# One graph-attention and experts kernel on Trainium2: strides of the attention's values, work moved at three borders between stages, larger register loads

## The chip, the cores and the metric

The kernel runs on one core of one Trainium2 chip, as one launch. The metric is the device time of that launch in microseconds (us). The time before is 2967.96 us, the median of three runs (2966.99 to 2968.54).

The core's engines are named as in the profile: PE (TensorE matmul), PEld (TensorE weight load), DVE (VectorE), ACT (ScalarE), POOL (GpSimd), SP (SyncE, which only issues DMAs here). SBUF is the on-chip memory that the engines read, PSUM the one that PE writes to. Each engine works through its own instructions in order and waits on semaphores for the others.

## What is computed

Two layers on 4096 rows of 256 channels. Cut to what matters:

```python
# layer 0
x = x + gat(layernorm(x), adj, W0, a1, a2)          # 4 heads of 64 channels
h = layernorm(x)
for _ in range(30):
    h = h + 0.01 * tanh(h); h = h * sigmoid(h)
    h = layernorm(h) @ W.T + b
x = x + h
# layer 1: two attentions in a row, then 6 experts, the best 2 for each row
x = x + gat(gat(layernorm(x), adj, W1, A1), adj, W2, A2)
f = layernorm(x)
p = softmax(relu(f @ rw1 + rb1) @ rw2 + rb2)
top_w, top_i = top_k(p, 2); w = softmax(top_w)
x = x + sum_i w[i] * expert[top_i[i]](f)            # three matmuls with relu between

# gat, per head
e = leaky_relu(f1[:, None] + f2[None, :], 0.2)
out = elu(softmax(where(adj > 0, e, -inf)) @ h)
```

The three attentions are called layer 0, layer 1 and layer 2 below (tags g0, g1, g2).

## The kernel before

**Attention.** `attention()` runs three times. A softmax over exp(leaky_relu(f1 + f2)) is split by the sign of f1 + f2: on either side the exponential is a product of a row's factor and a column's, so the matmuls work on 0/1 masks as weights (fp8, `st` for edges with a positive sum, `below` for the others) and on *values*, which are the head's 64 channels times the column's factor, high and low halves in fp16, and the factor itself: 130 fp16 numbers. The rows of the graph are done in four chunks of eight tiles of 128, a chunk takes four heads, and a head takes eight steps of four column tiles. In each step ACT (L464) or DVE (L462) makes four signs, each of one column tile by the chunk's 1024 rows, DVE takes masks from them (L569, L575), and PE runs the matmuls at L521: for each of the 32 column tiles `j`, each of 8 row tiles and both parts, one weight load of a mask and one matmul of 130 columns over `values[:, j, h, part]`. That is 8192 for each attention. The order on DVE and ACT is written out by hand (L539).

The last argument of `attention()` is a pair: the stride between two rows of values in SBUF, in fp16 numbers (`2 * DV` is 130, so 260 bytes; 160 gives 320), and the stride between the two parts' sums in PSUM, in fp32 numbers. Before, it is (130, 130) in layer 0, (160, 130) in layer 1 and (130, 256) in layer 2. With 260 bytes, the second part of each pair starts at 4 past a multiple of 8 bytes.

Layer 0 also loads the adjacency, 64 pieces of 1 MB, makes its masks and stores them; layers 1 and 2 load the stored masks. Weights, `hs` and a column mean are prepared ahead of each attention (L125 to L155, L291 to L294, L430 to L435). There the mean is a matmul with a weight tile that holds 1/C, or the sums copied by POOL into a full tile (`xsb`, L432), in each of its columns.

**FFN.** 30 steps over 8 units of 512 rows make 240 slots, each working on six units at different stages: PE transposes (L869), DVE applies the last product's scale (L877) and thereby frees PE's banks, ACT does silu and halves (L893, L897), DVE the other half (L898), SP transposes the fp16 halves by DMA (L902), ACT does tanh (L907), POOL adds (L908) and takes the power for the norm's factor (L928), DVE takes statistics (L917, L919), PE multiplies (L937, L940). The order on PE, DVE, ACT and POOL is written by hand, that on SP is the planner's. The first eight slots also prepare the eight units: `measure` (DVE statistics), `rate` (ACT, then POOL's power at L760) and `init` (the scaling; L779 on DVE where it says True, else L782 on ACT). A table, `opening`, tells in which slot each comes. In mid-stage, at slots 32, 56, and so on, `load` or `load_apart` fetches each unit's rows of x1 again, 512 KB each, for the residual at the end. They need nothing but their buffer, and the planner put all eight on SP's queue at the opening, between the first transposes.

**Routing and experts.** `route(h)` works on one half of the rows: statistics (`over_std`, L101 to L106), normalised rows (L1114), which are also stored to `nd`, transposes and two small matmuls per group of 512 rows (L1101), then the ranking of the best two, the places of the rows in a list sorted by expert, and the list itself: `shift` (L1199), `seen`/`ex`/`expert` (L1238 to L1248, the expert of each tile), one-hot tiles (L1221, L1226) for a matmul that sorts, then `source` and `dest` (L1250 to L1260), from which POOL gathers and scatters. The weight sums `ws` come ahead of the list. The rows come through a ring of four buffers (L93). `route(0)` is done before the first tile of the experts, `route(1)` between tiles. The experts take 37 tiles of 128 rows for each half: gather (L1315), transposes (L1326), three matmul layers (L1354 twice, L1375), scatter (L1378). `fetch` copies the tile's first two weights with an index held in a register (L1346); the register is loaded from `expert` on PE, DVE and ACT for four tiles at a time (L1335). The end adds the two scattered results of each row to `acc`.

## Time and profile before

The profiled execution took 2983.79 us, and its span, from the first instruction to the last, is 2982.0 us at a mean granted clock of 0.98. That is 15.8 us above the median of the runs, so durations from the trace are of a slightly longer execution.

| Stage | From, us | To, us | What runs |
|---|---|---|---|
| layer 0, attention | 95.0 | 602.9 | 8192 matmuls at L521 |
| FFN, opening | 603 | 640 | first units, no full rhythm |
| FFN | 640 | 1600 | 3.92 us a slot |
| layer 1, attention | 1627.8 | 2108.7 | 8192 matmuls |
| layer 2, attention | 2161.1 | 2646.2 | 8192 matmuls |
| routing of the first half | 2646.5 | 2704.3 | until the first expert's matmul |
| experts | 2704.3 | 2956.4 | 74 tiles |
| end | 2956.4 | 2982.0 | last sums and stores |

Read the page from the top: the busy share of each engine over the whole span, then the slices, where each digit is the busy share of a fortieth of the span in tenths. The last field of a group's line is the idle time of its engine just before it, with what ended most of it. Times on PE are such that a matmul's own duration (219 ns for L521) overlaps with its neighbours; the step from one start to the next is what counts. The slices of PE's clock and of the DMA engines:

```profile
PEclk9999999989999999999999999999999999988998
DMA  9999885043333333333353032120302222142243
```

The clock is full nearly everywhere. The DMA engines are full only in the first sixth, where the adjacency is loaded, and half full about the end of the attentions.

### The profile page before, as it was taken

The page shows a single profiled execution, that of the slowest core. Times are in us where ns is not written, and L with a number is a line of the kernel's source. Part 1 is how long each engine was busy: PE and PEld are TensorE (multiplying, and loading weights), DVE is VectorE, ACT ScalarE, POOL GpSimd, SP SyncE. Part 2 cuts the span into 40 slices and gives each one's busy share as a digit, 9 for nine tenths or more (in the row PEclk, how much of TensorE's full clock was granted, in tenths as well). Part 3 has the DMA queues.
Part 4 walks back from the last instruction along what each step waited for, and adds up shares of the span by engine and source line. Part 5 has one row for each costly group of instructions (what it writes and reads, how often), then busy time and mean ns, then how long its engine had stood idle before and what let it go on. Part 6 is the DMA issues. An engine that isn't in the chain of part 4 may idle for free. (4 is left out here: it accounts for less than half of the span.)

```text
span 2982.0 us, 82665 instructions
## 1 busy us (share of the span) xinstructions
PE 2795.9 (94%) x33923; PEld 2553.5 (86%) x33923; DVE 2737.1 (92%) x5769; ACT 2463.9 (83%) x3125; POOL 1159.1 (39%) x1084
## 2 busy tenths in 40 slices
PE   7899999979999999999998999999899999977986
PEld 5799999968888888888887999999799999967885
DVE  7999999999999999999998899999889999976665
ACT  5799999978888888888877999999799999954332
POOL 3000000079999999999982000000300000015563
PEclk9999999989999999999999999999999999988998
DMA  9999885043333333333353032120302222142243
GB/s 281 274 258 242 230 234 159 25 126 69 68 69 68 68 67 70 68 67 70 68 110 119 26 99 72 49 87 27 108 27 94 66 94 94 31 141 93 79 165 133
DMA packets 484450, 320.07 MB, mean 107 GB/s; under 512 B 416589, under 2 KB 445418, under 8 KB 477930
## 3 DMA queue, kind: packets, MB, share of 16 engines
q1 hardware_dynamic: 474034, 290.27, 36.1%
q0 software_dynamic: 7104, 19.41, 2.1%
q8 instruction: 268, 4.39, 0.6%
q10 hardware_dynamic: 2936, 5.11, 0.5%
q14 instruction: 108, 0.88, 0.1%
HBM read 183.00 MB, written 52.04 MB: 79 GB/s over the span
## 5 line engine op out<-in xcount | busy, mean ns | idle before, releaser
L521 PE MATMUL acc<-vals,st 128*128 128x130 f16 x12288 | 1425.1, 219 | 39.0 <-DVE u L476 30.6
L521 PE MATMUL acc<-vals,below 128*128 128x130 f16 x12288 | 1424.7, 221 | 14.0 <-DVE below L575 13.2
L464 ACT ACTIVATE st<-f1b,nf 128x1024 int8<-128x1024 f32 x1265 | 1334.2, 1145 | 30.3 <-PE acc L521 19.8
L521 PEld LDWEIGHTS <-below 128*128 128x128 fp8e4 x12288 | 1185.9, 97 | 55.0 <-issue 42.6
L521 PEld LDWEIGHTS <-st 128*128 128x128 fp8e4 x12288 | 1207.2, 98 | 9.6 <-DVE st L569 7.8
L937 PE MATMUL po<-wT,zT 128*128 128x256 f32 x1920 | 576.2, 382 | 6.1 <-DVE y L877 3.5
L940 PE MATMUL po<-w,zT 128*128 128x256 f16 x3840 | 577.9, 273 | 0.5 <-DMA zT<-z 0.5
L908 POOL TENSOR_TENSOR th<-th,y 128x1024 f32<-128x1024 f32 x232 | 548.9, 2366 | 14.5 <-DVE z_st L917 0.4
L940 PEld LDWEIGHTS <-zT 128*128 128x128 f16 x3840 | 376.6, 98 | 161.7 <-DMA zT<-z 1.2
L575 DVE TENSOR_TENSOR below<-m,st 128x1024 int32<-128x1024 int32 x384 | 469.9, 1224 | 32.6 <-DVE st L569 0.9
L569 DVE TENSOR_TENSOR st<-st,m 128x1024 int32<-128x1024 int32 x384 | 466.8, 1216 | 0.2
L877 DVE SCALAR_TENSOR_TENSOR y<-po,z_rs,bias 128x256 f32<-128x256 f32 x928 | 384.3, 476 | 2.2 <-PE tp L869 0.7
L917 DVE BATCH_NORM_STATS2 z_st<-z 128x6 f32<-128x256 f32 x960 | 335.5, 412 | 0.0
L937 PEld LDWEIGHTS po<-wT,zT 128*128 128x128 f32 x1920 | 291.1, 192 | 15.6 <-issue 3.7
L893 ACT ACTIVATE z<-th 128x1024 f32<-128x1024 f32 x240 | 251.9, 1050 | 17.6 <-POOL th L908 16.8
L928 POOL TENSOR_TENSOR z_rs<-z_rs,mhalf 128x4 f32<-128x4 f32 x240 | 245.4, 1022 | 3.1 <-ACT z_rs L927 3.1
L907 ACT ACTIVATE th<-y 128x1024 f32<-128x1024 f32 x232 | 241.7, 1042 | 0.0
L924 ACT COPY zT<-tp 128x512 f32<-128x512 f32 x240 | 140.4, 585 | 90.6 <-PE tp L869 89.5
L462 DVE TENSOR_SCALAR st<-f1b,nf 128x1024 int8<-128x1024 f32 x271 | 201.0, 742 | 6.2 <-PE acc L521 6.2
L760 POOL TENSOR_TENSOR x_rs<-x_rs,mhalf 128x4 f32<-128x4 f32 x8 | 9.4, 1175 | 505.3 <-ACT x_rs L759 505.3
L1046 POOL IOTA along_i<- 128x512 int32 (+1 forms) x5 | 2.8, 557 | 485.8 <-PE acc L521 485.7
L439 POOL MEMSET hs<- 128x4 f32 x3 | 0.3, 103 | 485.9 <-DVE u L493 485.9
(263 smaller groups left out, 3158.5 us busy)
## 6 DMA issues: line engine op xcount, KB each, us to landing
ring<-in_adj_dram SPq DMA_DIRECT2D x64, 1024.0 KB
m<-edges SPq DMA_DIRECT2D x32, 1024.0 KB
f1b<-fd SPq DMA_DIRECT2D x48, 512.0 KB
edges<-m SPq DMA_DIRECT2D x16, 1024.0 KB
y<-yd SPq DMA_DIRECT2D x16, 512.0 KB
ew<-in_L_ffn_expert_w_dram SPq DMA_DIRECT2D x18, 256.0 KB
t<-in_x_dram SPq DMA_DIRECT2D x8, 512.0 KB
old<-in_x_dram SPq DMA_DIRECT2D x16, 256.0 KB
```

The lines of the kernel that those rows point to most:

```text
L464: nc.scalar.activation(out, f1, AF.Sign, bias=f2, scale=-1.0)
L521: nc.tensor.matmul(acc[:, i, part * apart_s : part * apart_s + 2 * DV], masked[part][:, at_i // TR, s, rows], values[:, j, h, part], start ...
L569: nc.vector.tensor_tensor(above, above, whole, OP.bitwise_and)
L575: nc.vector.tensor_tensor(below, whole, above, OP.bitwise_xor)
L877: nc.vector.scalar_tensor_tensor(t[:, r, :] if end else y[:, g * G + r, :], po[:, r, :], rstd[:, r : r + 1], t[:, r, :] if end else bias, ...
L893: ins = nc.scalar.activation(z, th.pop(u), AF.Silu, scale=0.01)
L907: nc.scalar.activation(th[at], was, AF.Tanh, scale=0.01)
L908: ins = (nc.gpsimd if at else nc.vector).tensor_tensor(th[at], th[at], was, OP.add)
L917: nc.vector.bn_stats(st[:, r, :], z[:, r, :])
L928: nc.gpsimd.tensor_tensor(rs[u], rs[u], mhalf, OP.pow)
L937: nc.tensor.matmul(po[:, r, :], src[:, r * P : (r + 1) * P], wT, start=True, stop=False)
L940: nc.tensor.matmul(po[:, r, :], src16[:, part * G + r, :], w16[:, other, :], start=False, stop=(part == 1 and other == 1),)
```

## The change

- Values in layer 0 have a stride of 132 numbers (264 bytes). Layer 2 gets layer 1's pair (160, 130): 320 bytes, and sums 130 apart instead of 256.
- The mean is kept as one column and broadcast where it is a weight tile. The copy `xsb` on POOL is gone; the matmul at L435 reads the sums by a broadcast.
- FFN opening: `init` of units 4 and 5 goes from DVE in slots 2 and 3 to ACT in slots 3 and 4, `rate` of both one slot earlier.
- The eight loads in mid-stage are made to follow the L898 of the slot before.
- Routing: the second half's rows are loaded straight into `acc`, two of the four loads before `route(0)`, and the statistics of these two are done in `route(0)`'s last two turns. `seen`, `ex` and `expert` come after `source` and `dest`, DVE's order in `route(0)` is as written, and the tiles `ew`, `acc` and `ws` are allocated in another order. With these, the planner now puts the weight sums later.
- Registers are loaded for 4, 17 and 16 tiles of each half instead of ten times: 6 loads on each engine instead of 20.

As further effects of the planner's order, SP issues four mask loads of layer 2 earlier, two signs on ACT and three mask operations on DVE come earlier there, and POOL's first power in the routing comes behind its integer tables.

```diff
-    mean = const.tile([P, P], F32, name="mean")
-    nc.gpsimd.memset(mean, 1.0 / C)
+    share = const.tile([P, 1], F32, name="mean")
+    nc.gpsimd.memset(share, 1.0 / C)
+    mean = share.to_broadcast([P, P])
...
-                    xsb = prep.tile([P, KC, P], F32, name="xsb")
-                    nc.gpsimd.tensor_copy(xsb, xt[:, :, None].to_broadcast([P, KC, P]))
                     pt = small_ps()
                     for k in range(KC):
-                        nc.tensor.matmul(pt[:, :C], xsb[:, k, :], w[:, k, :C], start=(k == 0), stop=(k == KC - 1))
+                        nc.tensor.matmul(
+                            pt[:, :C], xt[:, k : k + 1].to_broadcast([P, P]), w[:, k, :C], start=(k == 0), stop=(k == KC - 1)
+                        )
...
         {k: functools.partial(many, *v) for k, v in side.items()},
+        (132, 2 * DV),
     )
...
+        halved = []
         units = FFN_STEPS * NG
         opening = {
-            0: [(init, 2)],
-            1: [(rate, 4), (rate, 5), (init, 3, True)],
-            2: [(init, 4, True)],
-            3: [(init, 5, True), (measure, 6)],
-            4: [(rate, 6), (measure, 7)],
-            5: [(init, 6), (rate, 7)],
+            0: [(init, 2), (rate, 4), (rate, 5)],
+            1: [(init, 3, True)],
+            3: [(init, 4), (measure, 6)],
+            4: [(rate, 6), (init, 5), (measure, 7)],
+            5: [(rate, 7), (init, 6)],
             6: [(init, 7)],
         }
...
             if 0 <= g < NG and part == 0:
-                if g < NG // 2:
-                    load(g)
-                else:
-                    load_apart(x1d, g)
+                ins = load(g) if g < NG // 2 else load_apart(x1d, g)
+                follows(ins, halved[0], "in mid-stage, when the queue has room")
...
+                halved[:] = [lower]
                 zT16[u] = work.tile([P, 2 * G, P], F16, name="zT16", bufs=4)
                 nc.sync.dma_start_transpose(zT16[u], z16.rearrange("p s r c -> p (s r c)"))
...
-            (2 * DV, 256) if n else (160, 2 * DV),
+            (160, 2 * DV),
...
+        def rest(g):
+            return acc[:, (NGH + g) * G : (NGH + g + 1) * G, :]
+
+        def measure_other(g):
+            early[g] = over_std(rone, rest(g), f"_{g}")
...
             def load(g):
-                if h * NGH + g not in ahead:
-                    load_ahead(x3d, h * NGH + g, runs_of)
-                rows[g] = ahead.pop(h * NGH + g)
+                if h:
+                    rows[g] = rest(g)
+                    if g in early:
+                        stds[g] = early.pop(g)
+                    else:
+                        nc.sync.dma_start(rows[g], runs_of(x3d, NGH + g))
+                else:
+                    rows[g] = ahead.pop(g)
...
+                if not h and g >= NGH:
+                    measure_other(g - NGH)
...
-            seen = rone.tile([P, T, E - 1], F32, name="seen")
...
-            nc.vector.tensor_copy(expert[h], ex)
             lst = rone.tile([P, T, 2], F32, name="lst")
...
             nc.vector.tensor_copy(dest[h], df)
             yield
+            seen = rone.tile([P, T, E - 1], F32, name="seen")
...
+            nc.vector.tensor_copy(expert[h], ex)
...
+            for g in range(2):
+                nc.sync.dma_start(rest(g), runs_of(x3d, NGH + g))
             steps = route(0, turned, bank)
-            for _ in range(4):
-                next(steps)
+            with tc.manual_schedule(engines={mybir.EngineType.DVE}):
+                for _ in range(4):
+                    next(steps)
...
-            for _ in steps:
-                pass
+            with tc.manual_schedule(engines={mybir.EngineType.DVE}):
+                for _ in steps:
+                    pass
...
-                n = min(4, T - t)
+                n = 4 if t == 0 else min(-(-(T - 4) // 2), T - t)
```

More of the change, by code (lines that the diff above doesn't have):

```diff
@@ L92, in load_ahead, with over_std @@
         turns[0] += 1
-        queue.dma_start(t, view(src, g))
         ahead[g] = t
-    def over_std(pool, src):
+        return queue.dma_start(t, view(src, g))
+    def over_std(pool, src, mark=""):
         st = pool.tile([P, G, 6], F32, name="ln_st")
-        mv = pool.tile([P, G, 2], F32, name="ln_mv")
+        mv = pool.tile([P, G, 2], F32, name=f"ln_mv{mark}")
         for r in range(G):
@@ L103, in over_std @@
             nc.vector.bn_aggr(mv[:, r, :], st[:, r, :])
-        rstd = pool.tile([P, G], F32, name="ln_rstd")
+        rstd = pool.tile([P, G], F32, name=f"ln_rstd{mark}")
         nc.vector.tensor_scalar(rstd, mv[:, :, 1], EPS, None, op0=OP.add)
@@ L293, in greatest @@
                     pt = small_ps()
-                    nc.tensor.matmul(pt[:, : 2 * H], mean[: 2 * H], dm, start=True, stop=True)
+                    nc.tensor.matmul(pt[:, : 2 * H], share[: 2 * H].to_broadcast([2 * H, P]), dm, start=True, stop=True)
                     nc.vector.tensor_copy(mb[:, 0, :], pt[:, H : 2 * H])
@@ L740, in gnn_ffn_kernel, with load @@
     x1, measured, rates = {}, {}, {}
-    def load(g, queue=nc.sync):
-        if g not in ahead:
-            load_ahead(x1d, g, queue=queue)
+    def load(g):
+        ins = load_ahead(x1d, g)
         x1[g] = ahead.pop(g)
+        return ins
     def measure(g):
@@ L836, in load_apart @@
             x1[g] = hold.tile([P, G, C], F32, name="x1")
-            nc.sync.dma_start(x1[g], rows_of(src, g))
+            return nc.sync.dma_start(x1[g], rows_of(src, g))
         for g in range(4, NG):
@@ L1025, in gnn_ffn_kernel @@
         bT = one.tile([P, NB], F32, name="bT")
-        acc = one.tile([P, NT, C], F32, name="acc")
-        ws = one.tile([P, 2, NT], F32, name="ws")
         bsel = [one.tile([P, T, 2 * KC], F32, name=f"bsel{h}") for h in range(2)]
@@ L1031, in gnn_ffn_kernel @@
         source = [one.tile([P, T], I32, name=f"source{h}") for h in range(2)]
-        ew = [one.tile([P, E, KC, C], F32, name=f"ew{i}") for i in range(3)]
+        ew = [one.tile([P, E, KC, C], F32, name=f"ew{i}") for i in (2, 1, 0)][::-1]
+        acc = one.tile([P, NT, C], F32, name="acc")
+        ws = one.tile([P, 2, NT], F32, name="ws")
         b3 = one.tile([P, E, C], F32, name="b3")
@@ L1078, in over @@
             return t[:, :, None].to_broadcast([P, n, m])
+        early = {}
+        def rest(g):
+            return acc[:, (NGH + g) * G : (NGH + g + 1) * G, :]
+        def measure_other(g):
+            early[g] = over_std(rone, rest(g), f"_{g}")
         def route(h, turned, bank):
@@ L1094, in route @@
                     load(g + 2)
-                if g < NGH:
+                if g < NGH and g not in stds:
                     stds[g] = over_std(rwork, rows[g])
@@ L1238, in route @@
                 yield
-            seen = rone.tile([P, T, E - 1], F32, name="seen")
-            nc.vector.tensor_tensor(
-                seen,
-                along[:, :T, None].to_broadcast([P, T, E - 1]),
-                first[:, None, 1:].to_broadcast([P, T, E - 1]),
-                OP.is_ge,
-            )
-            ex = rone.tile([P, T], F32, name="ex")
-            nc.vector.tensor_reduce(ex, seen, axis=AX.X, op=OP.add)
-            nc.vector.tensor_copy(expert[h], ex)
             lst = rone.tile([P, T, 2], F32, name="lst")
@@ L1261, in route @@
             yield
+            seen = rone.tile([P, T, E - 1], F32, name="seen")
+            nc.vector.tensor_tensor(
+                seen,
+                along[:, :T, None].to_broadcast([P, T, E - 1]),
+                first[:, None, 1:].to_broadcast([P, T, E - 1]),
+                OP.is_ge,
+            )
+            ex = rone.tile([P, T], F32, name="ex")
+            nc.vector.tensor_reduce(ex, seen, axis=AX.X, op=OP.add)
+            nc.vector.tensor_copy(expert[h], ex)
             ohe = rone.tile([P, T, E], F32, name="ohe")
```

## The prediction

> **What bounds the kernel now.** I read the page first, then the busy time per stage, then two stages closely. The page says that no one engine is the answer for the whole:

> ```profile
> PE 2795.9 (94%) x33923; PEld 2553.5 (86%) x33923; DVE 2737.1 (92%) x5769; ACT 2463.9 (83%) x3125; POOL 1159.1 (39%) x1084
> ...
> L464 ACT ACTIVATE st<-f1b,nf 128x1024 int8<-128x1024 f32 x1265 | 1334.2, 1145 | 30.3 <-PE acc L521 19.8
> ...
> L940 PEld LDWEIGHTS <-zT 128*128 128x128 f16 x3840 | 376.6, 98 | 161.7 <-DMA zT<-z 1.2
> ```

> So it has to be read by stage. The stage view (columns: stretch, length, busy us of PE, PEld, DVE, ACT, POOL with counts, granted clock, DMA share, GB/s) for layer 0's attention, the FFN's opening, a steady FFN stretch, layer 2's attention, the routing, the experts:

> ```profile
> 95.00:603.00 508.00, 483.52 (x8192) 477.77 (x8192) 489.16 (x554) 480.30 (x491) 8.31 (x12) 0.99 0.72 198
> 603.00:640.00 37.00, 20.50 (x108) 14.57 (x106) 34.75 (x100) 27.09 (x44) 24.22 (x24) 0.72 0.59 164
> 1000.00:1040.00 40.00, 40.00 (x288) 32.76 (x287) 39.92 (x134) 35.09 (x52) 38.54 (x32) 1.00 0.33 72
> 2161.00:2646.00 485.00, 476.01 (x8188) 473.90 (x8188) 449.76 (x495) 446.94 (x452) 0.00 (x0) 0.99 0.21 64
> 2646.00:2704.00 58.00, 23.00 (x132) 15.13 (x130) 42.18 (x156) 18.54 (x27) 19.85 (x38) 0.68 0.56 193
> 2704.00:2956.00 252.00, 237.64 (x1739) 219.22 (x1737) 160.79 (x490) 97.31 (x233) 145.56 (x146) 0.99 0.33 107
> ```

> Layer 2 is PE's (476 of 485). Layer 0 has three engines near 485 of 508, and in its middle ACT is full (50.00 of 50 between 250 and 300 us). The opening is DVE's (34.75 of 37), and routing has PE idle for 35 of 58 us behind small serial DVE work. Experts are PE's again.

> **The strides (layers 0 and 2).** L521's matmuls alone, same columns, PE and PEld only; the second line is layer 1 (values at 320 bytes), the third layer 2 (260 bytes):

> ```profile
> 200.00:300.00 100.00, 96.36 (x1657) 95.45 (x1654) 1.00 0.89 245
> ...
> 1850.00:1950.00 100.00, 98.96 (x1741) 98.58 (x1739) 1.00 0.20 64
> ...
> 2300.00:2400.00 100.00, 99.25 (x1714) 98.76 (x1712) 1.00 0.26 81
> ```

> The step is 98.96/1741 = 56.8 ns at 320 bytes and 99.25/1714 = 57.9 at 260. At 260 bytes the two matmuls of a pair start at multiples of 4 and of 8 bytes in turn; from the starts in the trace the one takes 59.45 ns to the next, the other 55.84: 115.28 a pair, against 113.32 in layer 1. Layers 0 and 2 are alike there, though their sums stand 520 and 1024 bytes apart in PSUM, so the sums' stride that layer 2 gets costs nothing.
> *Layer 2* gets layer 1's form. Its heads run 29.97 us each, layer 1's 29.54; DVE and ACT have at most 28.5 of work a head. 16 x 0.43 = 6.9, so **-7.0**. Ends: -4.2 (the two whole loops, 485.1 less 480.9 us, if layer 1's waits come too) and -8.0 (4096 pairs x 1.96 ns).
> [...]
> *Layer 0* gets 264 bytes: every start a multiple of 8, not of 64, a form that no row shows. Layer 2's steps depend on nothing but 4 against 8, so I take 264 as good as 320 (ends 0 and 1.96 ns a pair). But ten of 16 heads last 31 to 33 us, which is ACT's 28.8 signs x 1.04 plus 1.8; they stay. The other six can give 0.5 each at most, with DVE at 29.6 to 30.6 in four of them: **-1.5** (0 to -4).

> **FFN opening.** Before, DVE does the scaling of units 4 and 5 itself:

> ```profile
> 617.05 3.37 DVE L779 TENSOR_SCALAR x<-x,x_rs,x_nm 128x256 f32<-128x256 f32 x4
> ...
> 630.02 1.62 DVE L877 SCALAR_TENSOR_TENSOR y<-po,z_rs,bias 128x256 f32<-128x256 f32 x4
> ```

> First column start, second length. Two such blocks (3.37 + 2.10) leave DVE, and L877, which frees PE's banks (PE waits 3.5 us for it), can come 3 to 5 us sooner. ACT takes them at 2.06 each, and its slot becomes 3.7 + 2.06 + 0.3 = 6.1 us against DVE's old 5.1 to 5.9, for about four slots: it gives back some 2. Two POOL rates come a slot earlier and lie in POOL's idle time. I take **-2.5** (+1 to -5).

> **Row loads in mid-stage.** Eight loads of 512 KB leave the opening, where SP issued them between the first transposes, and come one per 24 slots, each right before a transpose on SP's queue. A slot is 3.92 us; its transpose holds the DMA engines for about 1.4 (share 0.33), so 2.5 are free, and 512 KB at the 290 GB/s that this queue reaches take 1.8. PE waits for zT 1.2 us in the whole run. The new wait of SP (for the L898 of the slot before) has the next transpose behind it, which waits for a later L898 anyway. **0**; if the cover is gone, each load delays one transpose by up to 2 us, +16 at the worst.

> **Means as one column, xsb.** L435's weights are read from the sums directly. It waited for ACT, not for POOL's copy of 1.33 us, which hid beside it; a broadcast fp32 column already loads in 198 ns at L341 against 192 for a full tile at L305. Layer 2's opening ends with 4.7 us of waiting for `below` (DVE L575), which is prepared by DVE alone; neither edit touches it. **0** (-0.5 to +0.5).

> **Routing.** Up to 2683.9 the order is nearly kept; POOL's first power is moved behind its iotas, 2.2 us later, and the normalised rows, transposes and ping-pong behind it follow: +1.9. SP gets two 512 KB loads ahead of the expert weights; they wait for the last x3d rows and freed buffers, as the first expert weight did, with one nd write and all weights behind them: 3 us of queue, with 10 us free before the first gather. Then comes the chain to the gather's indices:

> ```profile
> 2683.93 0.34 DVE L1240 TENSOR_TENSOR seen<-along,first 128x185 f32<-128x185 f32 x1
> ...
> 2697.09 0.17 DVE L1259 TENSOR_SCALAR source<-sf 128x37 int32<-128x37 f32 x1
> ...
> 2696.88 1.01 POOL L106 TENSOR_TENSOR ln_rstd<-ln_rstd,mhalf 128x4 f32<-128x4 f32 x1 [33.16 <-DVE sf L1258]
> 2698.15 1.54 POOL L1315 DMA_INDIRECT gx<-nd,source  x1 [0.26 <-DVE ln_mv L103]
> ```

> Of these 13.2 us, `seen` to `expert` (0.9), sel and bsel (2.1), three copies of weights and the second half's statistics (2 to 3) move behind the indices; parts of them overlap: -2.8. The weight sums at the front move away, -0.6. The gather no longer stands behind L106 (-0.8), and what follows it saves 0.5. Statistics of two groups come into the loop's last turns, where DVE waits for PE. Sum **-2.8** (+2 to -6).

> **Experts.** A tile takes 2.87 us of PE; 74 tiles are 212 of the 252 us, another 13 are the second half's routing, the rest stalls. One group of that routing can now run before the first tile, in PE's idle time (-2.1), and the statistics of two groups leave the path (-0.5). Register loads fall from 20 to 6 on PE, DVE and ACT; L1335's rows show a median of 346 ns on DVE and 310 on ACT. 14 x 0.35 = 4.8 us leave DVE; about 2 of that stood before a tile: **-4.5** together (0 to -8). [...] In the trace one register takes 323 ns and four take 346 on DVE, 8 ns more each, so 17 should take 0.45. [...]

> **Sum.** -7.0 - 1.5 - 2.5 + 0 + 0 - 2.8 - 4.5 = -18.3. The profiled execution took 2983.8 us with a span of 2982.0, 15.8 above the median of 2967.96; this cuts from both alike: span about 2964, median **about 2950 us** (0.6% faster). A measurement of this kernel can tell 0.2%, about 6 us, from no change.

> **Rivals.**
> - *Only layer 2 carries* (0.22): the opening turns ACT-bound, routing gives +1.9 and takes it back, tiles meet the same stalls. For it: every other part moves work between engines that are each near full. Against: routing has idle time on all. -7 to -10: 2959.
> - *Layer 0 gains as layer 2 does* (0.15): its ACT heads would have to be paced by PE. For: PE's 483.5 of 508. Against: ACT at 50.00 of 50. -6.5 more: 2943.
> - *Slower* (0.08): the steady FFN falls into another rhythm. Its slots take 3.92 us (PE 40.00, DVE 39.92, POOL 38.54 of 40, no slack anywhere), while those just after the opening ran at 3.80, so the pace depends on how the units stand to each other, and the opening is what sets this. A slot of 4.03 us or more, 0.11 x 225 = 25 us, makes it slower; at 4.05 it is 2979. Against: the order of a steady slot is unchanged.
> - *The stride doesn't do what it says* in layer 0 (64-byte starts needed): 2951, inside the forecast.

> **How the numbers follow.** The forecast holds 0.55, with 2943 to 2957 of its own. The range 2937 to 2964 takes in layer 0's case and most of the first rival. Faster (below 2962): 0.55 + 0.15 + 0.12 of the first rival = 0.82; same: its other 0.10; slower: 0.08.

> **What would show it.** L521's step in layers 0 and 2 at 56.7 ns (57.9 in layer 0 would refute 264 bytes); layer 2's loop near 478 us; layer 0's still over 500 with ACT full; PE's wait for L877 in the opening gone; zT waits still about 1 us; `source` some 18 us behind the last lg (2697.1 against 2675.6 now); the large register loads under 0.6 us. A steady slot other than 3.92 us, zT waits of more than 5 us, or register loads of 3 us would make the prediction wrong.

## The result, and the profile after

The changed kernel takes **2959.28 us** (median of 15 runs, 2952.40 to 2963.02), the kernel before in the same rounds 2967.03 (2964.74 to 2971.78). The ratio is 0.9971, 95% interval [0.9963, 0.9979]: 7.75 us or 0.29% faster. The forecast was 2950, with 2943 to 2957 around it and an outer range of 2937 to 2964: the time lies in the outer range, but the change brought only two fifths of the 18.3 us that the sum had. The profiled execution took 2959.31 us, with a span of 2957.4.

That span is 24.6 us under the one shown of before, three times what the runs differ by. The experiments show why: of two chips on which the kernel before was profiled again, one spends some 17 us more in the experts alone, and the first profile has that mark. The experts' 251.7 us of before are therefore no measure. Layers 1 and 2, the FFN and the routing agree from chip to chip (480.9 and 481.0, 485.1 twice, 3.92 us a slot twice, 58.2 twice); layer 0's loop took 503.9 to 511.4 us from one profile to the next, whatever the kernel, so the 3.7 us by which it is shorter here are no measure either.

The page after, the same three lines (busy and share; two groups of section 5 with busy, mean ns, idle before them):

```profile
PE 2788.3 (94%) x33923; PEld 2546.6 (86%) x33923; DVE 2734.9 (92%) x5761; ACT 2467.3 (83%) x3133; POOL 1159.8 (39%) x1083
...
L465 ACT ACTIVATE st<-f1b,nf 128x1024 int8<-128x1024 f32 x1265 | 1333.2, 1142 | 30.3 <-PE acc L522 23.7
...
L941 PEld LDWEIGHTS <-zT 128*128 128x128 f16 x3840 | 376.2, 98 | 161.0 <-DMA zT<-z 0.9
```

PE has 7.6 us less of busy time, most of it layer 2's. The wait for zT did not grow (0.9 us against 1.2): the loads in mid-stage delay no transpose that PE waits for. By stage, in the order shown before (layer 0, opening, steady FFN, layer 2, routing, experts), with the same columns (stretch, length, busy us of PE, PEld, DVE, ACT, POOL with counts, granted clock, DMA share, GB/s):

```profile
94.00:599.00 505.00, 479.98 (x8190) 474.58 (x8191) 489.59 (x554) 480.29 (x491) 8.30 (x12) 0.99 0.72 199
599.00:636.00 37.00, 21.87 (x126) 15.79 (x124) 32.73 (x98) 34.37 (x58) 27.02 (x27) 0.77 0.37 79
1000.00:1040.00 40.00, 40.00 (x289) 32.87 (x287) 39.91 (x137) 34.50 (x52) 38.52 (x32) 1.00 0.44 83
2154.00:2634.00 480.00, 470.51 (x8190) 467.68 (x8189) 450.34 (x496) 444.66 (x451) 6.00 (x20) 0.99 0.21 65
2634.00:2688.00 54.00, 26.70 (x141) 16.99 (x139) 43.35 (x161) 17.15 (x27) 13.98 (x20) 0.71 0.60 207
2688.00:2930.00 242.00, 232.88 (x1729) 218.49 (x1727) 162.00 (x485) 98.80 (x233) 148.10 (x145) 0.98 0.34 111
```

In the opening DVE fell from 34.75 to 32.73 and ACT rose from 27.09 to 34.37 of 37. A steady FFN stretch is what it was. Layer 2 needs 480 us instead of 485. L522 (L521 before) alone, layers 0, 1 and 2:

```profile
200.00:300.00 100.00, 95.97 (x1653) 95.19 (x1651) 1.00 0.88 246
1850.00:1950.00 100.00, 98.97 (x1741) 98.58 (x1739) 1.00 0.19 60
2300.00:2400.00 100.00, 99.08 (x1735) 98.34 (x1733) 1.00 0.31 97
```

Layer 2 has layer 1's density now: 99.08/1735 = 57.1 ns, and from start to start 56.66 where PE runs on. **Layer 0 has not changed**: 95.97/1653 = 58.1, as 96.36/1657 before, and from start to start again 55.84 and 59.4 in turn.

The routing's chain to the gather's indices, its first line as it was before and then two lines of after; and the register loads, PE's as they were before and then those of after in the queues of the three engines (shortest, median and longest in ns, first and last start):

```profile
2683.85 0.17 DVE L1199 SCALAR_TENSOR_TENSOR shift<-first,ends 128x6 f32<-128x6 f32 x1
...
2670.02 0.17 DVE L1215 SCALAR_TENSOR_TENSOR shift<-first,ends 128x6 f32<-128x6 f32 x1
...
2681.11 0.15 DVE L1265 TENSOR_SCALAR source<-sf 128x37 int32<-128x37 f32 x1
```

```profile
L1335 PEldq TENSOR_LOAD <-expert x20: 312/332/519, 2685.6 to 2945.3; - x20
...
L1355 ACTq TENSOR_LOAD <-expert x6: 319/1674/3591, 2682.9 to 2875.3; - x6
L1355 DVEq TENSOR_LOAD <-expert x6: 359/1364/3808, 2683.0 to 2876.3; - x6
L1355 PEldq TENSOR_LOAD <-expert x6: 351/1443/4207, 2683.0 to 2874.5; - x6
```

From `shift` to `source` it is 11.1 us instead of 13.2 (2683.85 to 2697.09). The loads are the surprise: shortest, median and longest are 0.35, 1.4 and 4.2 us on PE, where before the median was 0.33. 6 loads take 12.05 us of PE's queue, 20 took 6.98.

### The profile page after: what moved, and what is told of

Same layout as the page of the kernel before. It is cut to its first block, busy times and chain, and to the rows that moved or that the text cites. A ratio compares the mean times of both kernels' runs of the same rounds, so it can differ in the third digit from the quotient of the medians.

```text
span 2957.4 us, 82630 instructions
## 1 busy us (share of the span) xinstructions
PE 2788.3 (94%) x33923; PEld 2546.6 (86%) x33923; DVE 2734.9 (92%) x5761; ACT 2467.3 (83%) x3133; POOL 1159.8 (39%) x1083
## 5 line engine op out<-in xcount | busy, mean ns | idle before, releaser
L522 PE MATMUL acc<-vals,st 128*128 128x130 f16 x12288 | 1416.3, 220 | 38.6 <-DVE u L477 31.1
L522 PE MATMUL acc<-vals,below 128*128 128x130 f16 x12288 | 1416.0, 221 | 13.3 <-DVE below L576 12.6
L465 ACT ACTIVATE st<-f1b,nf 128x1024 int8<-128x1024 f32 x1265 | 1333.2, 1142 | 30.3 <-PE acc L522 23.7
L522 PEld LDWEIGHTS <-below 128*128 128x128 fp8e4 x12288 | 1195.0, 97 | 55.4 <-issue 48.4
L522 PEld LDWEIGHTS <-st 128*128 128x128 fp8e4 x12288 | 1206.1, 98 | 8.7 <-DVE st L570 6.9
L877 DVE SCALAR_TENSOR_TENSOR y<-po,z_rs,bias 128x256 f32<-128x256 f32 x928 | 384.4, 476 | 2.2 <-PE tp L869 0.7
```

The source lines that it names most:

```text
L465: nc.scalar.activation(out, f1, AF.Sign, bias=f2, scale=-1.0)
L522: nc.tensor.matmul(acc[:, i, part * apart_s : part * apart_s + 2 * DV], masked[part][:, at_i // TR, s, rows], values[:, j, h, part], start ...
L877: nc.vector.scalar_tensor_tensor(t[:, r, :] if end else y[:, g * G + r, :], po[:, r, :], rstd[:, r : r + 1], t[:, r, :] if end else bias, ...
```

## The experiments

Three batches, each on one chip, always beside the kernel before. A label with a_ is an edit of the changed kernel, one with b_ of the kernel before; "best" puts parts of the change on the kernel before. Ratios are those of the measurement with their intervals, and can differ a little from the quotient of the two medians. "Routing" is from layer 2's last matmul to the first one of the experts, "experts" from there to PE's end, both from the profiles.

| Kernel | Batch | Time, us | Before there | Ratio, 95% interval | Layer 2's loop | Routing | Experts |
|---|---|---|---|---|---|---|---|
| b_again (one run) | 1 | 2985.28 | 2986.29 | | 485.1 | 58.2 | 253.9 |
| a_regs4 | 1 | 2969.67 | 2986.29 | 0.9949 [0.9937, 0.9961] | 479.3 | 54.2 | 251.2 |
| a_align (one run) | 1 | 2982.65 | 2986.29 | | 477.9 | 55.4 | 263.0 |
| a_open | 1 | 2985.53 | 2986.29 | 0.9999 [0.9991, 1.0007] | 478.1 | 53.8 | 264.7 |
| after_again | 2 | 2957.88 | 2967.90 | 0.9969 [0.9957, 0.9981] | 478.9 | 54.7 | 240.9 |
| a_regs8 | 2 | 2952.12 | 2967.90 | 0.9941 [0.9928, 0.9955] | 479.5 | 54.4 | 232.8 |
| a_regs_al | 2 | 2953.97 | 2967.90 | 0.9951 [0.9937, 0.9964] | 479.0 | 54.8 | 237.0 |
| b_route | 2 | 2960.10 | 2967.90 | 0.9975 [0.9966, 0.9984] | 485.2 | 55.3 | 232.9 |
| b_again2 (one run) | 3 | 2963.20 | 2968.32 | | 485.1 | 58.2 | 236.7 |
| b_l2 | 3 | 2961.62 | 2968.32 | 0.9978 [0.9969, 0.9987] | 478.2 | 58.2 | 236.8 |
| a_regs_off | 3 | 2957.97 | 2968.32 | 0.9967 [0.9956, 0.9978] | 479.5 | 54.0 | 239.2 |
| best | 3 | 2951.32 | 2968.32 | 0.9939 [0.9925, 0.9953] | 479.4 | 55.5 | 231.3 |

### The kernel before again: b_again and b_again2

No edit.

> The kernel before, unchanged, for a second profile. The first profiled execution was 16 us above the median of the runs. Theory A (the profile itself makes small stalls longer at the register loads, one every four or five tiles): again 2980 to 2986 us, with the experts' 28 or so longer tiles, 35 us in all. Rival B (that execution was an outlier somewhere else, such as in layer 0): about 2968, and layer 0's loop near 504 us as after the change, not 507.9.

> The kernel before once more, for a profile on the same chip as the three below. What took longer on the first batch's chip lay in the experts. Theory: attentions and FFN as always (508, 481, 485 us; slots 3.92), and routing plus experts, from layer 2's last matmul to PE's end, take 295 to 298 us where the kernel takes 2968, and 310 to 312 where it takes 2986. Rival: the chips differ in every stage alike.

Both theories of the first were wrong: profiling adds nothing, since the plain runs took 2986 there too, and layer 0 was 508.0 us. The second settled it: routing and experts together took 294.9 us, where 312.1 was read on batch 1's chip (its layer 0 was 504.1, not the expected 508). These are the experts of batch 1 and batch 3, the same program:

```profile
2703.00:2957.00 254.00, 237.07 (x1738) 219.22 (x1736) 160.15 (x491) 96.75 (x233) 145.39 (x146) 0.99 0.33 106
```

```profile
2698.00:2935.00 237.00, 232.04 (x1738) 218.04 (x1736) 163.49 (x491) 98.16 (x233) 146.29 (x146) 0.99 0.35 114
```

and who PEld waited for in them, in us, times, longest:

```profile
PEld ph L1354 <- DVE h L1367: 10.1, 9, 1.7
PEld ph L1354 <- issue: 10.1, 14, 2.0
```

```profile
PEld ph L1354 <- DVE h L1367: 4.1, 4, 1.5
PEld ph L1354 <- issue: 2.2, 9, 0.3
```

The work is alike; the stalls differ, half of them ("issue") with nothing in the trace that ends them. In layers 1 and 2 (480.9 and 485.1 us on one chip, 481.0 and 485.1 on the other) and the FFN (3.92 us a slot) there is none of it. The granted clock of the experts is 0.99 on both. What makes batch 1's chip slower there isn't settled. So experts are compared inside a batch, or between batches 2 and 3, where the kernel before took 2967.90 and 2968.32.

### Register loads: a_regs4, after_again, a_regs8, a_regs_al, a_regs_off

```diff
-                n = 4 if t == 0 else min(-(-(T - 4) // 2), T - t)       # 4, 17, 16
+                n = min(4, T - t)                                      # a_regs4
+                n = 4 if t == 0 else min(9 if t == 28 else 8, T - t)   # a_regs8
+                n = 4 if t == 0 else 16 if t == 4 else T - t           # a_regs_al: 4, 16, 17
+                n = 1 if t == 0 else min(4, T - t)                     # a_regs_off
```

> The changed kernel with registers loaded for four tiles at a time, as before (20 loads on each engine, not 6). My prediction's step (a load costs 0.35 us, hardly more for more registers): 2 to 5 us slower than the changed kernel, 2961 to 2964. Theory after seeing the trace (loads of 16 and 17 take 1.3 to 4.2 us on each engine, and stop three engines; the small ones were hidden): 3 to 8 us faster, 2951 to 2956.

> The changed kernel itself, timed beside the three below on one chip. On the chip of the first batch the kernel before took 2986 us and not 2967, and variants with the large register loads gained nearly nothing there. Theory (large loads cost 13 us in the routing and experts, the small ones did not): 2 to 7 us faster than the kernel before, routing and experts at 316 to 319 us. Rival (the first batch's chip was peculiar): 0.9971 again, routing and experts near 296 us.

> The changed kernel with register loads of 4, 8, 8, 8 and 9 for each half (10 loads on each engine; every start a multiple of 4 tiles, 16 bytes). If a load costs about 0.2 us for each register: 1.6 us each, and the time stands between the changed kernel's and that with fours. If the cost comes only from loads that start off 16 bytes, as the 16 registers from tile 21 do: under 0.8 us each, and the time is that with fours or 1 to 3 us better.

> The changed kernel with loads of 4, 16 and 17 (starting at tiles 4 and 20, both multiples of 16 bytes) in place of 4, 17 and 16 (starting at 4 and 21). In the changed kernel's trace 17 registers from tile 4 took 1.3 to 2.1 us and 16 from tile 21 took 3.4 to 4.2. If the start decides: both now 1.2 to 2 us, and the kernel is 4 to 8 us faster than the changed one. If it is the number of loads, or the tile where it falls: the second load again above 3 us, and no faster.

> The changed kernel with register loads of 1, then 4 at a time, so that every load of four starts 4 bytes past a multiple of 16. Theory (an aligned four is one access of some 0.3 us, single registers cost about 0.25 each): each load of four takes 0.9 to 1.1 us instead of 0.34, and the kernel is 3 to 10 us slower than with aligned loads of four or eight. Rival (long loads are slow for their length, not their start): 0.34 us each, no slower.

On batch 1's chip, fours made the changed kernel gain 16.6 us where a_open, with the large loads, gained nothing. Some 3.8 us of that are a_open's table of the opening (below); the experts alone are 251.2 us with fours against 263.0 (a_align) and 264.7 (a_open) with the large loads. On batch 2's chip the gap is smaller but plain: 2952.12 with eights, 2957.88 with the change's loads, experts 232.8 against 240.9. There the rival of after_again was right, and the theory drawn from batch 1 alone was not: 0.9969, with routing and experts at 295.6 us. My step was wrong in sign. Fewer loads brought nothing either: 10 aligned loads of eight (a_regs8, 232.8) and 20 of four (b_route, the same code in the experts, 232.9) are alike.

What sets a load's price shows in single loads on PE: 16 registers from tile 21 (the change), 17 from tile 20 (a_regs_al), 4 from a tile one past a multiple of 4 (a_regs_off), 8 from tile 12 (a_regs8; the time in ns stands three times since it is one load):

```profile
L1355 PEldq TENSOR_LOAD <-expert x1: 4085/4085/4085, 2764.3 to 2764.3; - x1
```

```profile
L1355 PEldq TENSOR_LOAD <-expert x1: 1540/1540/1540, 2761.9 to 2761.9; - x1
```

```profile
L1355 PEldq TENSOR_LOAD <-expert x1: 997/997/997, 2743.7 to 2743.7; - x1
```

```profile
L1355 PEldq TENSOR_LOAD <-expert x1: 602/602/602, 2724.9 to 2724.9; - x1
```

The length alone doesn't decide: 17 registers cost less than 16, and four cost 1.0 us or 0.33. Nearly all durations on PE fit one count, an estimate from these loads: about 0.3 us for a first access and 0.25 for each further one, where **a load that starts at a multiple of 16 bytes in `expert` counts one access for every four registers, and a load that starts elsewhere counts one for each register, to its end**: 16 from tile 21 are 16 accesses (4.1 us measured), 17 from tile 20 are five (1.5), four off the boundary are four (1.0), eight on it two (0.6). Aligned fours inside a load didn't help: 16 from tile 21 would then be seven accesses, some 1.8 us by this count, and took 4.1. "Access" is a name for what fits, since the trace shows durations only. Exceptions are the first load of each run (0.5 to 0.6 us) and single longer ones, such as fours of up to 1.8 us on DVE in b_again2. The trace of before had only aligned fours and single ones at the end, one access each by this count (0.33 and 0.31 us), and I read that as "hardly more for more registers".

What such a load does, in after_again's timeline (start, length, then the idle time before it in brackets):

```profile
2766.13 0.62 ACT L1366 COPY w<-ew 128x512 f32 x1 [3.07 <-PE pt L1346]
...
2768.33 0.53 DVE L1366 COPY w<-ew 128x512 f32 x1 [2.25 <-issue]
2768.41 1.63 PEld L1374 LDWEIGHTS ph<-h,w 128*128 128x128 f32 x8 [3.23 <-issue]
```

All three stand until their loads are through, which began at 2762.5 to 2764.4 and ended at 2765.93 (ACT), 2768.14 (DVE) and 2768.38 (PE). "issue" is the mark on PE and DVE: nothing in the trace but the load ends their wait. ACT's row names a matmul, but its wait ends 0.20 us behind its load. In all, PEld's waits under "issue" at the experts' L1374 add to 6.8 us in after_again, the longest 3.2, and to 1.5 in a_regs8, the longest 0.3.

The expectations: a_regs4, 3 to 8 us faster, was exceeded on its slower chip (12 to 13.5 us in the experts). a_regs8, under 0.8 us a load if only the start counts: 0.55 to 0.60 for most loads of eight. a_regs_al, 4 to 8 us over the changed kernel: 3.9 us by the times, with the second load at 1.3 to 1.6 us. a_regs_off, 3 to 10 slower than aligned loads: 5.4 to 6.7 (10.35 gained, where a_regs8 gained 15.78 in batch 2 and best 17.0).

### Strides: a_align and b_l2

```diff
-            (160, 2 * DV),
+            (144, 2 * DV) if n else (136, 2 * DV),      # a_align, on the changed kernel
```
```diff
-            (2 * DV, 256) if n else (160, 2 * DV),
+            (136, 256) if n else (160, 2 * DV),         # b_l2, on the kernel before
```

> The changed kernel with values at 272 bytes in layer 1 (a multiple of 16, not of 32) and 288 in layer 2 (of 32, not of 64); layer 0 stays at 264. Theory: a start off 16 bytes makes every second step slow (59.4 ns), so both read 56.66 ns a step, and loops of 481 and 480 us. Rival: only multiples of 64 bytes are quick, so both read a mean of 57.64 and loops of about 485 us; or of 32, then layer 1 alone is slow.

> The kernel before with one number changed: layer 2's values at 272 bytes instead of 260, its sums still 256 apart; the order of all engines is the same. Theory: steps of 56.66 ns, layer 2's loop at 478 to 480 us instead of 485, and 5 to 7 us faster in all, the largest single gain of the change. Rival (layer 2 is held by DVE or ACT once PE is quicker): steps quicker, but the loop gains under 3 us.

a_align, layers 1 (272 bytes) and 2 (288 bytes), and b_l2, layer 2 (272 bytes):

```profile
1850.00:1950.00 100.00, 98.97 (x1741) 98.58 (x1739) 1.00 0.19 60
2300.00:2400.00 100.00, 99.23 (x1740) 98.62 (x1738) 1.00 0.30 94
...
2300.00:2400.00 100.00, 98.90 (x1737) 98.41 (x1735) 1.00 0.25 81
```

All are as dense as 320 bytes: 56.66 ns from start to start where PE runs on. Of the strides run, the multiples of 16 bytes (272, 288, 320) are quick (56.66 ns), and 8 past one (264, 57.63 ns in the mean) is as slow as 4 past one (260, 57.64). a_align's loops were 481.2 and 477.9 us, so its rivals of 32 and 64 bytes are out. It isn't each start by itself: with 260 bytes half the first matmuls of a pair begin 8 past a multiple of 16, counted from the tile's start (those of the heads with odd numbers), and take the same 55.8 ns as the others; the second of the pair pays in every head (59.4 to 59.5 ns to the next). Whether the distance between the two matters or something else in the stride wasn't separated.

b_l2 changes one number and no engine's order: 6.7 us faster by the times, its loop 478.2 us against 485.1 in b_again2. That is the whole of the sum's largest term (-7.0 predicted). The rival is out. The stride didn't need the mean as one column, which frees 508 bytes: b_l2 keeps the full tile. No run has 320 bytes in layer 2 beside the full tile.

### Opening: a_open

```diff
-            0: [(init, 2), (rate, 4), (rate, 5)],
-            1: [(init, 3, True)],
-            3: [(init, 4), (measure, 6)],
-            4: [(rate, 6), (init, 5), (measure, 7)],
-            5: [(rate, 7), (init, 6)],
+            0: [(init, 2)],
+            1: [(rate, 4), (rate, 5), (init, 3, True)],
+            2: [(init, 4, True)],
+            3: [(init, 5, True), (measure, 6)],
+            4: [(rate, 6), (measure, 7)],
+            5: [(init, 6), (rate, 7)],
```

> The changed kernel with the opening's table of before (units 4 and 5 scaled on DVE in slots 2 and 3); the loads stay in mid-stage. If the table brought the 3.8 us that the first slots lost: 2962 to 2964. Rival: the mid-stage loads, now out of the opening's queue, brought it, and the table nothing: 2958 to 2960.

The times can't answer, since the experts, with the large loads, took 264.7 us on this batch's chip and not 241.9. The trace does. The first five steps of L937 from one slot to the next add to 30.05 us before (6.84, 7.55, 6.36, 5.28, 4.02), 26.24 after (the second is 3.92), and 30.05 in a_open. Over all profiles they add to 26.2 to 26.7 in the eight with the new table and to 30.0 to 30.1 in the six without. So the table brings 3.4 to 3.8 us, and the mid-stage loads bring nothing here by themselves. Nor do they cost anything later: from the sixth slot's product to the last slot's it is 916.84 us in each of the fourteen profiles. In the trace of after, L877 of the first unit stands at 622.62, 9.0 us behind the first product, against 12.6 before:

```profile
622.62 1.62 DVE L877 SCALAR_TENSOR_TENSOR y<-po,z_rs,bias 128x256 f32<-128x256 f32 x4
```

and of PE's waits on a product at the opening (in us, times, longest), these two lines of before

```profile
PE po L937 <- DVE y L877: 3.5, 1, 3.5
PE po L937 <- ACT zT L924: 2.7, 3, 1.1
```

leave only one, for ACT:

```profile
PE po L938 <- ACT zT L925: 3.7, 3, 1.5
```

The 3.5 us for L877 are gone; in a_open, 3.3 of them are there.

### Routing alone, and the parts that gain together: b_route and best

b_route is the kernel before with the change's routing section and register loads of four. best is b_route plus these:

```diff
-                n = min(4, T - t)
+                n = 4 if t == 0 else min(9 if t == 28 else 8, T - t)
...
-            (2 * DV, 256) if n else (160, 2 * DV),
+            (136, 256) if n else (160, 2 * DV),
...
+                follows(ins, halved[0], "in mid-stage, when the queue has room")
```

and the change's table of the opening.

> The kernel before with the change's routing alone (rows straight into acc, early statistics, seen behind source, DVE's order, tiles' order), register loads of four as before; strides, means, opening and mid-stage loads as before. My prediction's routing part and two items of the experts: -2.8 - 2.6 = -5.4, so about 5 us faster. Rival (routing gives nothing of itself, the profile's difference is chance): within 2 us of the kernel before.

> The parts that gained, put on the kernel before: the changed routing with aligned register loads (4, 8, 8, 8, 9), the opening's table with the loads in mid-stage, layer 2's values at 272 bytes; means, layer 0's stride and the sums of layer 2 as before, so that layer 2's preparation keeps its old order. If the parts add: -8 (routing) - 4 (opening) - 6 (layer 2) = -18 to -20 us, 2 to 4 better than the changed kernel with these register loads alone (0.9941 of the kernel before). Rival: layer 2's later start in the changed kernel does not come from the means, and the time is that one again, -15 to -17.

b_route gains 7.8 us, more than the expected 5: routing 58.2 to 55.3, experts 236.7 (b_again2) to 232.9. Its rival is out. best takes **2951.32 us**, 17.0 under the kernel before, and is quicker than the changed kernel by about 7 on comparable chips. It falls into the range of its rival (15 to 17): the time from layer 1's last matmul to layer 2's first is 52.3 to 52.4 us in the five profiles without the mid-stage loads, b_route and b_l2 among them, and 53.1 to 54.1 in the nine with them, best (53.2) and a_open (53.1) among them. best has the full tile of means, so the means are not what moved it. No other part of the change is in all nine and in none of the five; how the mid-stage loads would change the order there, with two signs and a mask on DVE ahead of the values, wasn't tried.

## Why the prediction was right in its direction, and where its size failed

| Step | Predicted, us | Measured, us | From |
|---|---|---|---|
| layer 2's stride | -7.0 | -5.6 (alone -6.9) | loop, after; b_l2 |
| layer 0's stride | -1.5 | 0 | step unchanged |
| opening | -2.5 | -3.8 | five steps, after; a_open |
| mid-stage loads | 0 | 0 | zT waits, a_open |
| means, xsb | 0 | not seen | |
| layer 2's start | 0 | +0.7 | first profile after |
| routing | -2.8 | -3.5 | after_again against b_again2 |
| experts | -4.5 | +4.2 | after_again against b_again2 |
| sum | -18.3 | -8.0 | runs: -7.75 |

The outer range held the time, but not because the sum was right: one part of it, the experts, came out 8.7 us worse than forecast. Nor was the first rival right, though its 2959 is the time measured. It had only layer 2 carry; in fact the opening and the routing gained as well, and the experts lost. That agreement is luck. The table's sum lies near the runs' difference in part by luck too, since it mixes profiles: read from after_again alone, layer 2 is -6.2, its start +1.7, the opening -3.4 and the sum -7.2, while the runs of that batch gave -10.0.

- **The step that failed** is the register loads in the experts' sum: "In the trace one register takes 323 ns and four take 346 on DVE, 8 ns more each, so 17 should take 0.45." They took 1.3 to 2.2 us, and the 16 from tile 21 took 3.4 to 4.2. By the experts of after_again and a_regs8 the large loads cost 8.1 us (240.9 less 232.8), where the sum had them save about 2: 10 us, about all of the 10.3 that the sum was short of. The range given for the whole part, 0 to -8, doesn't hold its +4.2. I went by L1335's rows of before, though they went no further than four registers, all of which started at a multiple of 16 bytes.
- The other two items of the experts, one group's transposes and two groups' statistics, were right in sum: without the large loads the experts are -3.9 (a_regs8's 232.8 against 236.7) or -3.8 (b_route), predicted -2.6. How the two share it wasn't separated.
- Layer 2 was right in mechanism and size. Fifteen of its 16 heads took 449.6 us together with 260 bytes and 443.0 to 443.2 in every profile without: -6.6 to start from. The first head gives back 1.0 in after (36.5 us instead of 35.5) and took 34.9 to 36.5 in others; why wasn't tried.
- Layer 0: "I take 264 as good as 320" failed. The rival of the stride that does nothing there was right. Its loop lasted 503.9 to 511.4 us with 260 bytes (six profiles) and 504.2 to 509.8 with 264, so a single pair of profiles (507.9 and 504.2) shows nothing. The reason given, that the steps depend on 4 against 8 bytes, came from one slow form alone: with 264 the second of a pair starts at 8 and pays all the same (59.4 ns to the next). (Eleven heads, not ten, lasted 31 to 33 us.)
- Opening: right, and on the low side. ACT seems to have given back less than the 2 us I had taken off, which wasn't measured apart.
- Routing: the sum was nearly right by a different split, and so in part by luck. From `shift` to `source` 2.1 us went, in every profile with the new routing, not 2.8; `shift` came 0.2 to 1.8 us earlier behind layer 2's end (1.3 in after_again), not 1.3 later; and the gather still stands 1.0 us behind `source`: L106 was not what it had waited for.
- One reason given in a rival was misread: the slots just after the opening ran at 3.92 us like all others; there was no faster rhythm of 3.80, and the steady FFN never moved.
- Of the signs named, L521's step (layer 2), its loop (479.6 us), layer 0's loop over 500, the wait for L877 and that for zT came out. Layer 0's step did not, `source` stood 19.3 us behind the last lg and not 18 (21.5 before), and the large register loads were far over 0.6 us. Register loads of 3 us had been named as a sign of being wrong, and two on each engine took 3.4 to 4.2.

## What to carry to other kernels

A duration in a trace is shown for the form that stands there: before a load, a copy or a matmul is made longer or is moved, ask which sizes and starts the row has (here four registers from a multiple of 16 bytes, 0.33 us, where 16 from tile 21 then took 4.1), and for a form that it doesn't have keep a dearer price as the outer end until a run shows it. The register loads stand in no busy sum (PE's counts 33923 instructions with 20 of them and with 6), so look for such instructions in the queue rows and for "issue" behind them. And profile the old kernel again on the chip of the new one before two profiles are subtracted: here one program's experts took 253.9 us on one chip and 236.7 on another.
